# Four GNN layers on 64 graphs: recording the graphs as planned tasks, four in flight, with all compute engines tied to the planned order

## The chip, the cores and the metric

One core of a Trainium2 chip. The metric is the device time of one launch in microseconds (us); the executions of a kernel in one round agree within 0.4%, those of the kernel before within 0.6%, and each kernel was run four times or more beside the kernel before on the same chip. All runs quoted are of the fast state. TensorE is called PE in the profile, VectorE DVE, ScalarE ACT, GpSimd POOL and the sync queue SP.

## The reference, cut to what matters

Each of 64 graphs has 256 nodes with 512 features, a 256x256 adjacency and a node mask, all float32. Four layers follow each other, and each begins with a layer norm and a relu:

```python
h = max(layernorm(x), 0); x = x + w0 * (h @ Wv0)              # layer 0: w0 = softmax over nodes of a masked q.k sum
h = max(layernorm(x), 0); x = x + relu(att @ feats)           # layer 1: 8 heads; att = softmax over neighbours of
                                                              #   leaky_relu(e_self + e_neigh), masked by -1e10
h = max(layernorm(x), 0); x = x + relu(tanh(A*(Xc Xp^T)) Xp)  # layer 2: 8 heads
h = max(layernorm(x), 0); x = x + w3 * (h @ Wv3)              # layer 3: w3 = softmax over nodes again
```

The layers of one graph depend on each other, the graphs do not. So TensorE is fed by keeping several graphs in flight, each at another place of its four layers.

## The kernel before

Each graph is a Python generator. Three are in flight, and a loop lets each record a piece in turn. Pools hand out the tiles, and the scheduler then places every instruction by itself. The norm hops to GpSimd for the power -0.5, since VectorE does the rest of it; TensorE can transpose only when `hn` is there (cuts are marked `# ...`):

```python
def normed(xt):
    for c in range(NC): nc.vector.bn_stats(stats[:, c, :], xt[:, c, :])          # L165, VectorE
    for c in range(NC): nc.vector.bn_aggr(mv[:, c, :], stats[:, c, :])
    nc.vector.tensor_scalar(rstd, mv[:, :, 1], EPS, None, op0=OP.add)            # L169, VectorE, 128x2
    nc.gpsimd.tensor_tensor(rstd, rstd, power, OP.pow)                           # L170, GpSimd, 128x2
    for c in range(NC):                                                          # L173, VectorE
        nc.vector.tensor_scalar(hn[:, c, :], xt[:, c, :], mv[:, c, 0:1], rstd[:, c:c + 1],
                                op0=OP.subtract, op1=OP.mult)
    # ... TensorE transposes hn, ScalarE evicts it with a relu to ht
```

Layer 1: the sixteen row maxima, the sending of them, and then GpSimd's additions of the mask:

```python
for c in range(NC):
    for h in range(H):                                                           # L291, VectorE, 128x256 x16 a graph
        nc.vector.tensor_tensor_reduce(junk, en_b[:, h, :], neg[:, c, :], 1.0, -BIG, OP.add, OP.max, mx[:, c, h:h + 1])
    yield
# ... maxima transposed, sent to DRAM and broadcast to m_b
yield
for p in range(HP):
    for s in range(2):
        for j in range(NC):
            nc.scalar.activation(e[:, s, j, :], es_b[:, h, :], AF.Prelu, bias=..., alpha=0.2)
    nc.gpsimd.tensor_tensor(e, e, negt[:, None].to_broadcast([P, 2, NC, N]), OP.add)   # L340, GpSimd, 128x1024
    nc.vector.tensor_tensor(e, e, m_b[...], OP.subtract)                               # L341
    nc.scalar.activation(e, e, AF.Exp)
    # ... gather(): TensorE multiplies e by feats
    yield
```

## Time and profile before

| | before |
|---|---|
| median (range) | 5157.3 us (5156.8 to 5168.0) |
| TensorE busy, mean granted clock | 89%, 0.948 |
| VectorE, ScalarE, GpSimd busy | 52%, 33%, 24% |
| TensorE's waits for e (exponentials) and for hn (norms) | 257 and 113 us |

How to read it: TensorE is the bound, so only its idle time and its slow clock can be won. The prediction below shows those lines.

### The profile page before, as it was taken

What the parts mean: (1) busy time and instruction counts of PE and PEld (TensorE: products, weight loads), DVE (VectorE), ACT (ScalarE), POOL (GpSimd) and SP (SyncE); (2) the same over time, 40 slices, a digit from 0 to 9 for tenths busy, and PEclk for the clock granted to TensorE, in tenths of its full rate; (3) what the DMA queues carried; (4) which work ended last, traced back from release to release, by engine and by line L of the source; (5) the groups of instructions that cost most, each with busy time, mean ns of one, the idle gap of its engine ahead of it and who ended that gap; (6) DMA issues with size and microseconds to landing.
All of it is one profiled execution on the core that took longest, in us unless ns stands there. A gap on an engine that the chain in (4) does not pass through costs nothing.

```text
span 5153.0 us, 60457 instructions
## 1 busy us (share of the span) xinstructions
PE 4603.7 (89%) x22850; PEld 3120.2 (61%) x22850; DVE 2691.4 (52%) x7530; ACT 1679.7 (33%) x3333; POOL 1231.3 (24%) x1095
## 2 busy tenths in 40 slices
PE   4898998989999989989899999899898999899987
PEld 3665666666665656665666656566656666566665
DVE  3555555555555555555545555555555455555543
ACT  1323333233233233332332332333333323323322
POOL 1222222122122222221221222222212222222211
PEclk8999999999999999999999999999999999999988
DMA  4111211111112112111111121121111111111101
GB/s 121 61 56 53 72 37 72 62 63 56 57 52 72 60 49 72 40 69 64 61 56 59 50 72 60 49 72 40 69 64 61 56 64 48 69 64 45 65 29 37
DMA packets 99779, 306.88 MB, mean 60 GB/s; under 512 B 18016, under 2 KB 48800, under 8 KB 74912
## 3 DMA queue, kind: packets, MB, share of 16 engines
q1 hardware_dynamic: 74752, 261.65, 14.3%
q0 software_dynamic: 9216, 33.56, 1.7%
q10 hardware_dynamic: 15520, 7.80, 0.6%
q8 instruction: 181, 2.97, 0.2%
q14 instruction: 110, 0.90, 0.1%
HBM read 267.85 MB, written 35.13 MB: 59 GB/s over the span
## 4 chain that ended last, share of the span: by engine, by line
PE 38%; DVE 9%; POOL 4%; issue 4%; ACT 2%; DMA 0%; POOLq 0%; DVEq 0%; ACTq 0%
PE pf L187 9%; PE pv L187 9%; PE pz L433 5%; PE po L320 4%; POOL e L340 3%; PE pg L444 3%; PE pt L179 2%; DVE e L341 2%; DVE stats L165 1%; DVE junk L291 1%; PE pc L377 1%; DVE th L405 1%; ACT e L342 1%; PE pyt L391 1%; DVE xt L419 1%
## 5 line engine op out<-in xcount | busy, mean ns | idle before, releaser
L187 PE MATMUL pv<-wv_s,ht 128*128 128x512 f32 x2048 | 1005.8, 639 | 14.4 <-ACT ht L180 14.4
L320 PE MATMUL po<-feats,e 128*128 128x65 f32 x4096 | 574.4, 296 | 257.6 <-ACT e L342 257.0
L320 PEld LDWEIGHTS po<-feats,e 128*128 128x128 f32 x4096 | 549.0, 212 | 342.5 <-issue 216.9
L340 POOL TENSOR_TENSOR e<-e,negt 128x1024 f32<-128x1024 f32 x256 | 636.3, 2493 | 397.2 <-ACT e L338 311.3
L187 PEld LDWEIGHTS pv<-wv_s,ht 128*128 128x128 f32 x2048 | 403.5, 205 | 451.1 <-issue 426.0
L180 ACT ACTIVATE ht<-pt 128x512 f32<-128x512 f32 x512 | 287.2, 595 | 983.5 <-PE pt L179 982.8
L341 DVE TENSOR_TENSOR e<-e,m_b 128x1024 f32<-128x1024 f32 x256 | 362.6, 1431 | 376.9 <-POOL e L340 375.9
L338 ACT ACTIVATE e<-es_b,ec 128x256 f32<-128x256 f32 x1024 | 449.9, 495 | 46.5 <-PE po L320 37.8
L187 PE MATMUL pf<-w_s,ht 128*128 128x512 f32 x1024 | 452.3, 594 | 5.5 <-ACT ht L180 5.5
L433 PE MATMUL pz<-ht,m_s 128*128 128x256 f32 x2048 | 455.5, 381 | 0.7 <-ACT ht L180 0.7
L391 PE MATMUL pyt<-th,xp 128*64 128x256 f32 x2048 | 378.7, 404 | 66.9 <-ACT th L406 66.9
L433 PEld LDWEIGHTS pz<-ht,m_s 128*128 128x128 f32 x2048 | 387.6, 191 | 62.1 <-issue 10.4
L179 PE MATMUL pt<-ident,hn 128*128 128x128 f32 x2048 | 322.3, 302 | 113.2 <-DVE hn L173 112.9
L170 POOL TENSOR_TENSOR rstd<-rstd,power 128x2 f32<-128x2 f32 x256 | 199.0, 778 | 919.1 <-DVE mv L167 581.2
L406 ACT ACTIVATE th<-th 128x512 f32<-128x512 f32 x512 | 312.9, 623 | 305.8 <-DVE th L405 305.7
L405 DVE TENSOR_TENSOR th<-ps,adj_t 128x512 f32<-128x512 f32 x512 | 333.6, 683 | 103.3 <-PE ps L401 100.3
L179 PEld LDWEIGHTS pt<-ident,hn 128*128 128x128 f32 x2048 | 269.1, 160 | 193.3 <-issue 145.0
L342 ACT ACTIVATE e<-e 128x1024 f32<-128x1024 f32 x256 | 269.8, 1055 | 341.3 <-DVE e L341 339.5
L291 DVE CUSTOM_DVE_ANT_0 junk<-en_b,neg 128x256 f32<-128x256 f32 x1024 | 376.3, 420 | 4.5 <-DMA en_b<-er_d 3.0
L165 DVE BATCH_NORM_STATS2 stats<-xt 128x6 f32<-128x512 f32 x512 | 342.5, 678 | 56.2 <-POOL xt L331 51.1
L173 DVE TENSOR_SCALAR hn<-xt,mv,rstd 128x512 f32<-128x512 f32 x512 | 261.0, 548 | 172.1 <-POOL rstd L170 171.9
L331 POOL TENSOR_TENSOR xt<-xt,o 128x256 f32<-128x256 f32 x256 | 184.3, 727 | 611.5 <-DVE o L328 592.1
(88 smaller groups left out, 5239.6 us busy)
## 6 DMA issues: line engine op xcount, KB each, us to landing
en_b<-er_d SPq DMA_DIRECT2D x64, 1024.0 KB, 4.4
es_b<-er_d SPq DMA_DIRECT2D x64, 1024.0 KB, 6.7
m_b<-m_d SPq DMA_DIRECT2D x64, 1024.0 KB, 4.6
xt<-in_x_dram SPq DMA_DIRECT2D x64, 512.0 KB, 3.8
out_dram<-xt POOLq DMA_DIRECT2D x64, 512.0 KB, 3.2
adj_in<-in_adj_dram SPq DMA_DIRECT2D x64, 256.0 KB, 3.9
mask_in<-in_nodemask_dram SPq DMA_DIRECT2D x64, 128.0 KB, 8.1
w_n<-in_L_gnn_Wqk_dram ACTq DMA_DIRECT2D x16, 128.0 KB, 3.6
```

Source lines behind the costliest of these rows:

```text
L165: nc.vector.bn_stats(stats[:, c, :], xt[:, c, :])
L179: nc.tensor.transpose(pt[:, k * P:(k + 1) * P], hn[:, c, k * P:(k + 1) * P], ident)
L187: nc.tensor.matmul(p, ht[:, k, c * P:(c + 1) * P], w[:, k], start=(k == 0), stop=(k == KC - 1))
L291: nc.vector.tensor_tensor_reduce(junk, en_b[:, h, :], neg[:, c, :], 1.0, -BIG, OP.add, OP.max, mx[:, c, h:h + 1])
L320: nc.tensor.matmul(po[i][:, q, :], e[:, s, j, i * P:(i + 1) * P], feats[:, j, h, :], start=(j == 0), stop=(j == NC - 1))
L338: nc.scalar.activation(e[:, s, j, :], es_b[:, h, :], AF.Prelu, bias=ec[:, j, H + h:H + h + 1], alpha=0.2)
L340: nc.gpsimd.tensor_tensor(e, e, negt[:, None].to_broadcast([P, 2, NC, N]), OP.add)
L341: nc.vector.tensor_tensor(e, e, m_b[:, 2 * p:2 * p + 2, None, :].to_broadcast([P, 2, NC, N]), OP.subtract)
L342: nc.scalar.activation(e, e, AF.Exp)
L391: nc.tensor.matmul(pyt[s * U:(s + 1) * U, p % 2, :], xp[:, m, h * U:(h + 1) * U], th[:, s, m, :], start=(m == 0), stop=(m == NC - 1))
L405: nc.vector.tensor_tensor(th[:, s], ps[s], at, OP.mult)
L433: nc.tensor.matmul(pz[:, s, :], m3_s[:, k, d * P:(d + 1) * P], ht[:, k, :], start=(k == 0), stop=(k == KC - 1))
```

## The change

Its intent: let a planner, which knows about how long each step takes, decide what TensorE does next, so that with four graphs in flight a ready matmul is always at hand; and keep what it decided on TensorE, VectorE, ScalarE and GpSimd. Each graph is cut into tasks that name their predecessors, their steps (engine and length), the tiles taken and those given back. The core of the diff, with cuts:

```diff
-IN_FLIGHT = 3
-APART = 8
+IN_FLIGHT = 4
+BEHIND = 30.0
+PINNED = (mybir.EngineType.PE, mybir.EngineType.Activation, mybir.EngineType.DVE, mybir.EngineType.Pool,)
+    def issue(self, task, g, at):
+        # ... tiles are taken from the planner's own lists
+        task.run(*[t[2] for t in passing])
+        for i in traced[n:]:
+            if i.engine in PINNED:
+                if i.engine in self.last:
+                    self.tc.add_manual_dep(i, self.last[i.engine], ...NoSync...)
+                self.last[i.engine] = i.name
+        for engine, length in task.steps:
+            start = max(at, self.free[engine])
+            self.free[engine] = start + length
+    def run(self, graph, count):
+        # ... of all tasks whose predecessors are planned and whose tiles are there:
+        #     the one whose first step can start first; ties by graph and by the work left
+        @task(f"stats{layer}", after, [("V", 1.9), ("G", 0.75)])
+        @task(f"hn{layer}", f"stats{layer}", [("V", 1.1)], {"hn": 1})
+            @task(f"max{i}", f"<max{i - 1}" if i else "send neg", [("V", 2.0)], ...)     # four of these, four maxima each
+            @task(f"ea{p}", "wait negt" + ..., [("A", 2.0), ("G", 2.6)], ...)            # Prelu and GpSimd's addition
+            @task(f"eb{p}", f"ea{p} sendm", [("V", 1.21), ("A", 1.05)], ...)             # subtraction and exponential
-        nc.gpsimd.dma_start(out[b].rearrange("(c p) d -> p c d", p=P), xt)
+            nc.sync.dma_start(out[b].rearrange("(c p) d -> p c d", p=P), g["xt"])
```

## The prediction

> **What bounds the kernel now.** The page's first part gives the engines, its fourth the chain that ended last:
>
> ```profile
> PE 4603.7 (89%) x22850; PEld 3120.2 (61%) x22850; DVE 2691.4 (52%) x7530; ACT 1679.7 (33%) x3333; POOL 1231.3 (24%) x1095
> ...
> PE 38%; DVE 9%; POOL 4%; issue 4%; ACT 2%; DMA 0%; POOLq 0%; DVEq 0%; ACTq 0%
> ```
>
> TensorE is the bound and nothing else is near it; DMA is not on the chain. So the change can win only what TensorE loses. I read that from the timeline, in starts instead of ends, because ends are modelled:
>
> ```profile
> 2002.72 7.07 PE L433 MATMUL pz<-ht,m_s 128*128 128x256 f32 x32
> 2009.63 1.90 PE L320 MATMUL po<-feats,e 128*128 128x65 f32 x16
> 2011.36 1.04 PE L179 MATMUL pt<-ident,hn 128*128 128x128 f32 x8
> 2012.24 3.62 PE L444 MATMUL pg<-ht,zt 128*128 128x256 f32 x16
> ```
>
> From start to next start, undisturbed: pz 6.91 us for 32, po 1.73 for 16, eight transposes 0.88, pg 3.45. The same reading for every group gives a graph's full-speed work: pv of two layers 13.8, pf with w1a, w1b and w2 3.7 + 3.5 + 6.9, pz 6.9, pg 3.5, po 7.0, ps 4.3, pyt 4.1, all transposes into ht, xpt, y and adj 5.8, qk and first score 2.9, xc 1.9, small ones 0.9, together 65 us.
>
> The chain in order of time repeats every three graphs:
>
> ```profile
> 2226.28 8.76 PE pv L187 x16
> ...
> 2465.72 8.51 PE pv L187 x16
> ...
> 2701.79 8.23 PE pv L187 x16
> ```
>
> (2701.8 - 2226.3) / 6 = 79 us a graph. From 500 to 4900 us the windows view has TensorE busy 91%, so of 78.5 us some 71.3 are busy and 7.2 idle; the busy part is 6.4 us above the 65. That surplus is mostly clock, as windows of 3 us show (columns: stretch, its length, busy us of PE, PEld, DVE, ACT, POOL, then PEclk, DMA):
>
> ```profile
> 2088.00:2091.00 3.00, 1.55 (x15) 1.31 (x13) 2.99 (x7) 1.08 (x2) 0.00 (x0) 1.00 0.98 344
> 2091.00:2094.00 3.00, 0.29 (x2) 0.32 (x3) 2.28 (x10) 0.00 (x0) 0.69 (x1) 0.89 0.84 355
> 2094.00:2097.00 3.00, 2.31 (x6) 1.23 (x5) 3.00 (x16) 0.60 (x1) 0.00 (x0) 0.50 0.00 0
> 2097.00:2100.00 3.00, 3.00 (x5) 1.10 (x4) 2.97 (x19) 0.00 (x0) 0.36 (x1) 0.50 0.03 8
> 2100.00:2103.00 3.00, 3.00 (x11) 1.53 (x10) 1.64 (x5) 0.60 (x1) 0.92 (x2) 0.98 0.00 0
> ```
>
> A wait of 4.2 us (a transpose waiting for hn while VectorE works off y, two more normalisations and the row maxima) is followed by some 6 us at half clock. A mean clock of 0.948 means 10% of the span, some 540 us or 8.4 us a graph, at half; it costs up to 4 us a graph. So a wait is paid twice. The waits view names whom TensorE waits for:
>
> ```profile
> DVE e L341 <- POOL e L340: 375.9, 165, 4.9
> PE po L320 <- ACT e L342: 257.0, 123, 5.7
> PE pt L179 <- DVE hn L173: 112.9, 47, 8.6
> POOL out_dram L455 <- DVE xt L208: 712.7, 63, 24.7
> ```
>
> The exponentials of layer 1 (257 us) and the normalisations (113) are two thirds of its 549 us idle. The last line is GpSimd standing with a store at its head, unable to add the masks meanwhile.
>
> **What the Trainium skill says.** "TensorE: Matmul & The Clock Gate", part 1 on the clock gate: the array runs at full or half clock, half after an idle window of about 3.4 us. The windows above agree in kind. The same page, on engine queue depths: ScalarE and VectorE are strictly in order. So tying a compile-time order cannot speed an instruction; it decides who blocks whom. The store at GpSimd's head agrees. "Perfetto Trace Analysis", identifying the most-contended engine: matmul busy share is a poor measure of what is left. It agrees: 89% busy hides 6.4 us a graph. "DMA: Bandwidth & Descriptors", SWDGE vs HWDGE: plain transfers belong on the sync queue, whose descriptors hardware makes. Here the 64 issues took GpSimd 782 ns each.
>
> **The change, part by part.** Arithmetic is unchanged: no matmul, eviction or large transfer goes. A fourth graph enters, with four transposed adjacencies. The load broadcasts the node mask later, one memset of 127 ns a graph goes, and the store moves from GpSimd to the sync queue: 50 us of issue and most of the 713 us of standing leave GpSimd, which is 24% busy; alone worth little, since only waits for e pass through it.
>
> The large part is the order. A task puts all its instructions into the engines' orders when its first step is planned. An eviction is therefore fixed on VectorE when its matmul is issued, and VectorE-only work planned later stands behind it until that matmul ends. Before, the scheduler placed each instruction by itself. I listed the new order and walked three neighbouring graphs of its middle by hand, taking each group's undisturbed duration above and, for VectorE, the means of its rows (e 1.43 us or less, th 0.68, bn_stats 0.68, hn 0.55, four maxima 2.0), exponentials 1.06, GpSimd's e 2.5. This is an estimate, and leaves out most hand-over delays.
> - First graph: after the last po, VectorE has the division (1.2), stats of the newcomer (1.95), the y additions (1.4), two more stats (3.9) and half of hn (0.55): 9.0 us; TensorE has py, adj and y, 2.35 us. It stands 6.7 us. Later waits of 0.5 to 1.1 us; 70.5 us in all.
> - Second: the first subtraction of e stands on VectorE behind the eviction of the last w1b group, and po follows that group at once: 0.4 + 1.4 + 1.1 and hand-overs are 3.3 us of wait; 69 us.
> - Third: the last th stands behind a division and stats (1.8 us), then hn behind maxima (1.1), and po twice behind e; 75.5 us.
>
> The mean is 71.7 us: 65 of work and about 7 of wait. So the plan does not remove the waits; it breaks them up. The three have two waits long enough for half clock, against 90 half-clock stretches for 64 graphs before, over four for three graphs. I take 2 us a graph of clock loss (two stretches of 6 us, half of it lost, over three graphs) and 1.5 us for hand-overs, a choice: some 10 a graph on the path at 0.15. That gives 75.2 us. Start and end now take 5153 - 64 x 78.5 = 129 us; the setup is the same, with four graphs ready behind it, so I keep 100. Sum: 64 x 75.2 + 100 = 4910 us; I lean 30 us lower because the broadcasts, which the walk found with at least 4 us of slack, and the removed store may help: **4880 us**.
>
> **Rivals.**
> 1. VectorE's order becomes the bound. For: 52% busy, and 55% in a run of 4880 us (2691 / 4880); evictions block it while some 35 us of matmuls a graph run. Against: TensorE's groups without eviction there (pv, transposes, po, pyt) leave about 30 us for 29 us of VectorE-only work. If it tips, 78 us a graph: 5090, no gain.
> 2. Pinned orders are brittle: a broadcast later than planned, or a store ahead of a send in the sync queue (a load waits there for a store to land), stops VectorE and then all. For: four engines can't step around it. Against: row maxima came 11 to 15 us after their send in the walk, and about 7 are needed (1.4 + 4.4 + issue). If wrong, 2 to 4 us a graph more: 5040 to 5170.
> 3. TensorE fills: with four graphs a ready matmul nearly always exists, waits fall to 3 us, the clock stays full: 65 + 3 + 1.5 = 69.5, or 4550. For: long matmul stretches of two graphs interleave. Against: the walk's 6.7 us hole, where all four graphs stand at a layer boundary.
>
> **Range and chances.** The walk is good to some 2.5 us a graph, 160 us, mostly through clock and hand-overs: 4690 to 5060 at 8 in 10. Faster by 2% means under 5054: 0.87. Within 2%: 0.10, by the first or second rival. Slower: 0.03; it needs over 80 us a graph.
>
> **What would show it.** TensorE's matmul counts unchanged. Period near 75 us; mean clock about 0.97 (4 us of 75 at half); TensorE busy 91 to 94%. The wait of po for the exponentials falls well below 257 us; the wait of transposes for hn does not fall, and may exceed 113 us. GpSimd's wait for the store goes. If the clock reads 0.99 and the hn wait is short, the walk was too dark (third rival). If TensorE waits for evictions, or VectorE for broadcasts, the first or second rival took it.

## More of the kernel before

The kernel before read 5157 to 5172 us in the rounds, which were on different chips, so a difference between kernels of different rounds is good to some 15 us.

The next lines are from the views of two source lines of the kernel before; the three figures are the shortest, the median and the longest of one instruction, in ns.

```profile
L291 DVE CUSTOM_DVE_ANT_0 junk<-en_b,neg x1024: 403/418/2571, 93.2 to 5046.9; 128x256 f32<-128x256 f32 x171
L340 POOL TENSOR_TENSOR e<-e,negt x256: 2327/2360/3420, 97.5 to 5059.3; 128x1024 f32<-128x1024 f32 x128
```

A row maximum takes 418 ns and one addition of the mask 2360 ns. The longest maximum, 2571 ns, is an addition long. In the kernel before that happened to one of the 1024.

## The result, and the profile after

The changed kernel took 5066.9 us (5066.8 to 5068.1, four runs) against 5157.3: a ratio of 0.982, with an interval of 0.9803 to 0.9837. Ratios here are the mean time of one kernel's fast runs over that of the other's of the same rounds, so not quite the ratio of the medians quoted. That is 1.8% faster, and 187 us above the predicted 4880 and 7 us above the predicted range.

The page of the changed kernel, the lines that answer to the first ones of the prediction:

```profile
PE 4492.2 (89%) x22850; PEld 3094.1 (61%) x22850; DVE 3072.8 (61%) x7530; ACT 1698.9 (34%) x3333; POOL 1173.8 (23%) x969
...
PE 79%; DVE 17%; issue 2%; ACT 1%; DMA 1%; ACTq 0%; POOL 0%; DVEq 0%; POOLq 0%
```

TensorE has the same 22850 matmuls and is no fuller than before. VectorE has the same 7530 instructions and is busy for 381 us more (3073 against 2691). Nobody gave it work; its instructions became longer. (Its 17% of the chain can't be set against the 9% in the prediction: that chain reaches back only to 2178 us and covers 57% of its span.) The waits view (total us, times, longest):

```profile
PE tr L378 <- DVE hn L370: 397.6, 87, 13.5
PE acc L551 <- ACT pair L534: 64.0, 32, 10.4
```

The waits for exponentials fell from 257 to 64 us as meant, and those of the transposes for hn rose from 113 to 398. The gain was given back there: TensorE is idle for 573 us in all, where it was 549. The 90 us that the kernel did win lie in its busy time, 4492 us against 4604, and no run separates where they come from. The period can be read from the chain in order of time, in which one group (line L668) returns once a graph:

```profile
1687.12 6.91 PE tr L668 x32
...
4472.41 6.91 PE tr L668 x32
```

There are 36 graphs between the two, so 77.4 us a graph against 78.5 before and 75.2 predicted. (64 x 77.4 leaves some 112 us of the span for start and end.)

Which VectorE instructions grew? By form, the maxima, hn and the 128x2 addition ahead of the power, first before, then after; columns are busy us, mean ns, idle before:

```profile
L291 DVE CUSTOM_DVE_ANT_0 junk<-en_b,neg 128x256 f32<-128x256 f32 x1024 | 376.3, 420 | 4.5 <-DMA en_b<-er_d 3.0
L173 DVE TENSOR_SCALAR hn<-xt,mv,rstd 128x512 f32<-128x512 f32 x512 | 261.0, 548 | 172.1 <-POOL rstd L170 171.9 <-PE pt L179 0.2
L169 DVE TENSOR_SCALAR rstd<-mv 128x2 f32<-128x2 f32 x256 | 66.7, 261 | 3.0
```

```profile
L490 DVE CUSTOM_DVE_ANT_0 junk<-all,neg 128x256 f32<-128x256 f32 x1024 | 644.1, 684 | 0.0
L370 DVE TENSOR_SCALAR hn<-xt,mv,rstd 128x512 f32<-128x512 f32 x512 | 327.6, 682 | 13.5 <-POOL rstd L364 8.0 <-PE tr L378 5.2
L363 DVE TENSOR_SCALAR rstd<-mv 128x2 f32<-128x2 f32 x256 | 143.0, 559 | 8.9
```

Those three grew by 268, 67 and 76 us. The views of single lines (shortest, median, longest in ns) say how:

```profile
L490 DVE CUSTOM_DVE_ANT_0 junk<-all,neg x1024: 406/418/2587, 103.2 to 4943.5; 128x256 f32<-128x256 f32 x171
L526 POOL TENSOR_TENSOR pair<-pair,negt x256: 2327/2358/3337, 108.7 to 4936.7; 128x1024 f32<-128x1024 f32 x128
L359 DVE BATCH_NORM_STATS2 stats<-xt x512: 667/677/695, 4.9 to 5032.4; 128x6 f32<-128x512 f32 x171
```

The median maximum is unchanged at 418 ns. A count over the records of the trace gives 165 of the 1024 above 600 ns, some half of those near 2.5 us, where the kernel before has one. Every one of the 165 ends within 0.3 us of the end of a GpSimd instruction: 110 with an addition of the mask, 50 with the product `am` (L681, 1.44 us), 5 with others. bn_stats, with one tensor in, never changed. The timeline of the longest hole shows the meeting; these lines are from 2286 to 2301 us:

```profile
2293.36 2.33 POOL L526 TENSOR_TENSOR pair<-pair,negt 128x1024 f32<-128x1024 f32 x1
...
2293.55 2.17 DVE L363 TENSOR_SCALAR rstd<-mv 128x2 f32<-128x2 f32 x1
...
2296.58 2.36 POOL L526 TENSOR_TENSOR pair<-pair,negt 128x1024 f32<-128x1024 f32 x1
...
2296.67 2.55 DVE L490 CUSTOM_DVE_ANT_0 junk<-all,neg 128x256 f32<-128x256 f32 x1
2298.90 1.44 POOL L681 TENSOR_TENSOR am<-adj,mask_in 128x512 f32<-128x512 f32 x1
...
2300.68 1.54 PE L378 MATMUL tr<-ident,hn 128*128 128x128 f32 x6 [13.47 <-DVE hn L370]
```

An addition of two columns, 170 ns as a rule, begins 0.2 us after GpSimd's addition and ends with it, 2.17 us later. A maximum does the same 3 us on: it begins 0.1 us after an addition and ends 0.3 us after it. TensorE stands 13.5 us, and the windows of 3 us show what follows (columns as in the prediction):

```profile
2289.00:2292.00 3.00, 0.00 (x0) 0.00 (x0) 2.93 (x9) 3.00 (x9) 3.00 (x2) 0.71 0.12 46
2292.00:2295.00 3.00, 0.00 (x0) 0.00 (x0) 2.96 (x6) 0.68 (x2) 3.00 (x4) 0.50 0.00 0
...
2301.00:2304.00 3.00, 3.00 (x16) 3.00 (x15) 2.37 (x11) 1.66 (x3) 0.00 (x0) 0.52 0.49 131
2304.00:2307.00 3.00, 3.00 (x16) 2.66 (x15) 0.00 (x0) 0.73 (x2) 0.00 (x0) 1.00 0.00 0
```

VectorE reads as full (2.9 of 3 us) through the whole hole. A busy share does not tell an engine that works from one that stands inside an instruction. The three microseconds after the hole run at half clock; over the run, the mean clock fell from 0.948 to 0.934.

Two pages of the Trainium skill that I had not looked up for the prediction state the mechanism. "SBUF — State Buffer", in "SBUF: two separate sides", says that VectorE and GpSimd share a pair of ports under an exclusive lock: a VectorE instruction with two SBUF inputs, or one in a two-port mode, and a GpSimd instruction exclude each other for the whole of the one that began first. "GPSIMD Engine Reference", in its specifications, says that they share these interfaces. The trace agrees: 418 ns, or as long as what is left of a GpSimd instruction. Whether this is what cost the time is for the experiments.

### The profile page after: what moved, and what is told of

Read it like the earlier page. It is cut to its first block, busy times and chain, and to the rows that moved or that the text cites. A ratio compares the mean times of both kernels' runs of the same rounds, so it can differ in the third digit from the quotient of the medians.

```text
span 5065.2 us, 60793 instructions
## 1 busy us (share of the span) xinstructions
PE 4492.2 (89%) x22850; PEld 3094.1 (61%) x22850; DVE 3072.8 (61%) x7530; ACT 1698.9 (34%) x3333; POOL 1173.8 (23%) x969
## 4 chain that ended last, share of the span: by engine, by line
PE 79%; DVE 17%; issue 2%; ACT 1%; DMA 1%; ACTq 0%; POOL 0%; DVEq 0%; POOLq 0%
PE tr L309 20%; PE acc L309 16%; PE acc L551 10%; PE tr L668 9%; PE tr L378 5%; PE tr L618 5%; DVE junk L490 5%; PE tr L690 4%; PE acc L639 4%; DVE stats L359 3%; DVE hn L370 2%; PE tr L602 2%; DVE rstd L363 2%; DVE pair L621 1%; PE tr L587 1%
## 5 line engine op out<-in xcount | busy, mean ns | idle before, releaser
L309 PE MATMUL acc<-wv_s,ht 128*128 128x512 f32 x2048 | 978.5, 623 | 0.2
L490 DVE CUSTOM_DVE_ANT_0 junk<-all,neg 128x256 f32<-128x256 f32 x1024 | 644.1, 684 | 0.0
L309 PEld LDWEIGHTS acc<-wv_s,ht 128*128 128x128 f32 x2048 | 392.4, 201 | 411.4 <-issue 400.3
L526 POOL TENSOR_TENSOR pair<-pair,negt 128x1024 f32<-128x1024 f32 x256 | 612.7, 2407 | 118.1 <-issue 69.2
L551 PE MATMUL acc<-feats,pair 128*128 128x65 f32 x4096 | 544.0, 292 | 64.0 <-ACT pair L534 64.0
L551 PEld LDWEIGHTS acc<-feats,pair 128*128 128x128 f32 x4096 | 522.3, 208 | 118.2 <-ACT pair L534 81.7
L668 PE MATMUL tr<-ht,m_s 128*128 128x256 f32 x2048 | 463.8, 381 | 0.0
L309 PE MATMUL tr<-w_s,ht 128*128 128x512 f32 x1024 | 460.8, 595 | 0.1
L668 PEld LDWEIGHTS tr<-ht,m_s 128*128 128x128 f32 x2048 | 385.4, 191 | 73.1 <-issue 25.6
L524 ACT ACTIVATE pair<-all,ec 128x256 f32<-128x256 f32 x1024 | 419.7, 496 | 14.5 <-DMA all<-er_d 9.7
L370 DVE TENSOR_SCALAR hn<-xt,mv,rstd 128x512 f32<-128x512 f32 x512 | 327.6, 682 | 13.5 <-POOL rstd L364 8.0
```

The source lines that it names most:

```text
L309: nc.tensor.matmul(p, ht[:, k, c * P:(c + 1) * P], w[:, k], start=(k == 0), stop=(k == KC - 1))
L370: nc.vector.tensor_scalar(g["hn"][:, c, :], g["xt"][:, c, :], st["mv"][:, c, 0:1], st["rstd"][:, c:c + 1], op0=OP.subtract, op1=OP.mult)
L490: nc.vector.tensor_tensor_reduce(junk, g["all:en"][:, h, :], g["neg"][:, c, :], 1.0, -BIG, OP.add, OP.max, st["mx"][:, c, h:h + 1])
L524: nc.scalar.activation(e[:, s, j, :], g["all:es"][:, h, :], AF.Prelu, bias=st["ec"][:, j, H + h:H + h + 1], alpha=0.2)
L526: nc.gpsimd.tensor_tensor(e, e, g["negt"][:, None].to_broadcast([P, 2, NC, N]), OP.add)
L551: nc.tensor.matmul(po[i][:, h % 4, :], e[:, s, j, i * P:(i + 1) * P], feats[:, j, h, :], start=(j == 0), stop=(j == NC - 1))
```

## The experiments

The theories. **A**: the stretched VectorE instructions lie in TensorE's path at the layer boundary and cost the missing time. **B**: they lie beside it; the hole comes from VectorE's order alone, as the hand walk had it. **C**: tying four engines costs by itself. Later came **D**: tying costs only where the plan's lengths are false; and **E** against **F**, on where the rest of the gain came from.

### e1_later_adds: additions planned behind the maxima

```diff
-            @task(f"ea{p}", "wait negt" + (f" <ea{p - 1}" if p else ""), [("A", 2.0), ("G", 2.6)], ...
+            @task(f"ea{p}", "wait negt max0 max1 max2 max3" + (f" <ea{p - 1}" if p else ""), [("A", 2.0), ("G", 2.6)], ...
```

> One dependency more in the plan: the four Prelu-and-mask tasks of a graph wait for its four tasks of row maxima, so that GpSimd's additions can no longer run beside the same graph's maxima (exact result). Theory A (VectorE's instructions with two SBUF inputs stand still while a GpSimd addition runs; the maxima rose from 420 to 684 ns and that sits in the path at the layer boundary): maxima back below 460 ns, VectorE's busy time down from 3073 to about 2800 us, the wait of the transposes for hn from 398 to under 250 us, time 4850 to 4950 us. Theory B (the hole at the layer boundary comes from VectorE's order alone, as the walk had it): within 1% of 5067 us. Theory C (tying the engines is what hurts): within 1% of 5067 us.

Correct, and 4577.2 us: ratio 0.8853 (0.8830 to 0.8876), 490 us below the changed kernel. B and C had expected no change, and A some 120 to 220 us, so none of them is the whole of it. The same groups and waits, and the page's first line:

```profile
PE 4332.7 (95%) x22850; PEld 2977.7 (65%) x22850; DVE 2764.0 (60%) x7530; ACT 1699.4 (37%) x3333; POOL 1190.6 (26%) x969
```

```profile
L490 DVE CUSTOM_DVE_ANT_0 junk<-all,neg 128x256 f32<-128x256 f32 x1024 | 377.5, 425 | 0.1
```

```profile
PE tr L378 <- DVE hn L370: 111.8, 65, 7.4
```

The maxima are back at 425 ns, the waits for hn at 112 us, and the clock is 0.990. But this edit also gave a wholly new order, and that may be where the time went, so it does not rule B out. The next two runs keep the changed kernel's order.

### e2_short_add: the same orders, GpSimd's addition cut short

```diff
-                nc.gpsimd.tensor_tensor(e, e, g["negt"][:, None].to_broadcast([P, 2, NC, N]), OP.add)
+                nc.gpsimd.tensor_tensor(e[:, :, :, :2], e[:, :, :, :2], g["negt"][:, None, :, :2].to_broadcast([P, 2, NC, 2]), OP.add)
```

> GpSimd's mask addition is cut to 2 of 256 columns (wrong result on purpose); the orders of TensorE, VectorE and ScalarE are those of the changed kernel, instruction for instruction. Theory A: no VectorE instruction is stretched any more (maxima 420 ns, the 128x2 addition in rstd 261 instead of 559 ns, hn 548 instead of 682), VectorE busy about 2650 us, time 4780 to 4900 us. Theory B: 5000 us or more, since TensorE waits for the exponentials only 64 us in all and gains little from an earlier addition.

4875.7 us, 191 us below the changed kernel with TensorE's, VectorE's and ScalarE's orders instruction for instruction the same (the result is wrong). B had 5000 us or more, so it falls as the whole cause. The page's first line, the maxima and the waits for hn:

```profile
PE 4473.1 (92%) x22850; PEld 3089.2 (63%) x22850; DVE 2691.5 (55%) x7530; ACT 1696.3 (35%) x3333; POOL 617.7 (13%) x969
```

```profile
L490 DVE CUSTOM_DVE_ANT_0 junk<-all,neg 128x256 f32<-128x256 f32 x1024 | 405.6, 453 | 0.1
```

```profile
PE tr L378 <- DVE hn L370: 227.2, 65, 8.3
```

With the orders unchanged, VectorE's busy time fell from 3073 to 2692 us, so 381 us of stretching came from the long additions. That this is just what VectorE had gained is partly chance: 33 maxima still stand, up to 1493 ns, 31 of them beside the product `am`. The time won is half of the 381 us, so about half was in TensorE's path. A holds, with one reserve: GpSimd was also relieved of its additions, so e was there sooner. TensorE's waits for e did not shorten (68 us against 64).

### e3_one_input_max: maxima with one SBUF input

```diff
-                    nc.vector.tensor_tensor_reduce(junk, g["all:en"][:, h, :], g["neg"][:, c, :], 1.0, -BIG,
-                                                   OP.add, OP.max, st["mx"][:, c, h:h + 1])
+                    nc.vector.tensor_reduce(st["mx"][:, c, h:h + 1], g["all:en"][:, h, :], AX.X, OP.max)
```

> The row maxima read one SBUF tile instead of two (a plain reduction, wrong result on purpose); all else, the orders and GpSimd's additions too, as in the changed kernel. Theory A: the reductions take about 420 ns and are not stretched though the additions run beside them, time 4900 to 4980 us (268 of the some 410 us of stretching are the maxima's, part of it may pass to hn and rstd, which still meet the additions). Theory B: within 1% of 5067 us.

4995.7 us, 71 us below the changed kernel, just past the slow end of the expectation (4980). (Its maximum is over all nodes instead of neighbours; the softmax does not depend on it.) The outputs are right. Two lines of the single-line views and of the groups say both why it helped and why so little:

```profile
L490 DVE TENSOR_REDUCE mx<-all x1024: 399/408/421, 103.5 to 4872.0; 128x1 f32<-128x256 f32 x171
```

```profile
L370 DVE TENSOR_SCALAR hn<-xt,mv,rstd 128x512 f32<-128x512 f32 x512 | 393.6, 811 | 13.6 <-POOL rstd L364 8.0 <-PE tr L378 5.2
L363 DVE TENSOR_SCALAR rstd<-mv 128x2 f32<-128x2 f32 x256 | 160.6, 627 | 8.9
```

With the additions running as before, no one-input maximum of 1024 took over 421 ns. So it was the instruction with two inputs that stood. But hn went from 682 to 811 ns: what stood behind the maxima now meets the additions itself.

### e4_unpinned: no engine tied

```diff
-PINNED = (mybir.EngineType.PE, mybir.EngineType.Activation, mybir.EngineType.DVE, mybir.EngineType.Pool,)
+PINNED = ()
```

> The plan still allots the tiles and the order in which tasks are recorded, but no engine is tied to it: the scheduler of before places each instruction by itself. Theory C (pinned orders are brittle, tying all four engines costs): faster than 4990 us. Theories A and B: no faster than 5020 us; I expect 5050 to 5200 us.

4858.6 us, 208 us below the changed kernel; my expectation, 5050 to 5200, missed. In the changed kernel, tying costs 4%. The clash was not gone (maxima at 631 ns, hn at 900), but in the scheduler's order TensorE ran into it less: the waits for hn were 80 us, though some for other tiles came up. So C is right here. What remained was whether it is right in general.

### e5_later_unpinned: e1_later_adds with no engine tied

> The plan of e1_later_adds, with no engine tied. Theory D (tying costs only where the plan's lengths are wrong, as with the additions beside the maxima; with those apart the planned order is the better one): slower than e1_later_adds's 4577, 4620 to 4850 us. Theory C (tying costs by itself, as the 208 us between e4_unpinned and the changed kernel suggest): faster than 4560 us.

4690.6 us, 113 us above e1_later_adds. So tying loses 208 us with one plan and wins 113 with another that differs in one dependency, which fits D. Untied, the scheduler brings some of the clash back (maxima at 551 ns against 425), and how much of the 113 us is that clash was not tested: no untied run was free of it. That a tied order is as good as the lengths it was planned with is a reading of these two pairs, not shown.

### e8_short_replanned: e2_short_add, and the plan told of it

```diff
-            @task(f"ea{p}", "wait negt" + (f" <ea{p - 1}" if p else ""), [("A", 2.0), ("G", 2.6)], ...
+            @task(f"ea{p}", "wait negt" + (f" <ea{p - 1}" if p else ""), [("A", 2.0), ("G", 0.3)], ...
```

> e2_short_add (addition cut to 2 columns, wrong result on purpose), and the plan told so: the addition's length in it 0.3 instead of 2.6 us. So no addition stands ahead of a normalisation in GpSimd's order, in the plan or on the chip. Theory E (the 300 us by which e1_later_adds beats e2_short_add come from the plan's placing GpSimd's long additions ahead of the normalisations' power, which makes it hold hn back behind the maxima): 4560 to 4680 us. Theory F (they come from the sixteen Prelu activations or the buffers of the pairs, which e1_later_adds also moves): 4800 us or more.

4712.1 us (wrong result): 164 us below e2_short_add, between what E and F expected. The waits for hn are 111 us, as in e1_later_adds. So the plan made with long additions puts the norms late even where the additions stretch nothing, which fits E; but the edit changes the whole order, and it is not as fast as e1_later_adds.

### e9_rstd_vector: the norm without the hop to GpSimd

```diff
-            @task(f"stats{layer}", after, [("V", 1.9), ("G", 0.75)])
+            @task(f"stats{layer}", after, [("V", 2.1)])
-                nc.gpsimd.tensor_tensor(rstd, rstd, power, OP.pow)
+                nc.vector.reciprocal(rstd, rstd)
```

> The changed kernel with the normalisation's power replaced by a reciprocal on VectorE (wrong result on purpose: 1/v for 1/sqrt(v)), in the plan too. The additions still run beside the maxima. Theory E: hn no longer waits for GpSimd, time 4650 to 4850 us. Theory F: above 4950 us.

5229.9 us, slower than both kernels, where E had expected a large gain (1/v for 1/sqrt(v) is wrong; the power itself did not compile on VectorE). So taking the hop to GpSimd away does not help by itself. The groups suggest why:

```profile
L370 DVE TENSOR_SCALAR hn<-xt,mv,rstd 128x512 f32<-128x512 f32 x512 | 459.9, 948 | 0.0
L490 DVE CUSTOM_DVE_ANT_0 junk<-all,neg 128x256 f32<-128x256 f32 x1024 | 385.6, 431 | 0.0
```

In the new order the maxima are almost clear of the additions (431 ns), and hn is in their midst, at 948 ns. hn is what TensorE waits for, and those waits rose to 628 us. So the clash moved to a worse place. As the whole order changed too, what part of the 163 us above the changed kernel it cost is not shown, and E itself stays untested by this run.

### e6_three and e12_later_three: three graphs in flight

```diff
-IN_FLIGHT = 4
+IN_FLIGHT = 3
```

> The changed kernel with three graphs in flight in place of four. If the fourth graph earns its place, 5150 us or slower; if the holes come from the order alone, within 1.5% of 5067 us. The maxima would be stretched as before (over 550 ns), since nothing in the plan keeps them from the additions.

> e1_later_adds with three graphs in flight in place of four. If the fourth graph matters once the clash is gone: 4650 us or slower (e6_three lost 4% of the changed kernel); if three fill TensorE in a sound order: within 1.5% of 4577 us.

On the changed kernel 5288.4 us, 4.4% above it. On e1_later_adds 5124.9 us, 12% above it. Both plans lose by going to three graphs, but the second figure is not its worth alone: with three, the plan brought the additions beside hn again (1101 ns, maxima at 424), a clash that its one dependency does not exclude.

### e11_split_add: the addition cut into four

```diff
-                nc.gpsimd.tensor_tensor(e, e, g["negt"][:, None].to_broadcast([P, 2, NC, N]), OP.add)
+                for s, j in ((0, 0), (0, 1), (1, 0), (1, 1)): nc.gpsimd.tensor_tensor(e[:, s, j], e[:, s, j], g["negt"][:, j], OP.add)
```

> The changed kernel with each GpSimd addition of 128x1024 cut into four of 128x256 (exact result; the same orders on TensorE, VectorE and ScalarE). Theory A, as the runs have it so far: a VectorE instruction that meets an addition stands until that one instruction ends, so the stretched maxima shorten from 1.4 and 2.5 us to about 1 us or less, their mean falls from 684 to below 560 ns, and the time falls to 4920 to 5040 us although GpSimd's additions grow from 613 to some 720 us in all. If instead the two engines merely share bandwidth, the sum of stretching stays (mean near 684 ns) and the time does not fall.

Correct, and 4918.5 us: 148 us below the changed kernel, a little better than expected, with the same orders, although GpSimd's additions grew from 613 to 793 us:

```profile
L490 DVE CUSTOM_DVE_ANT_0 junk<-all,neg x1024: 411/423/1491, 103.2 to 4797.7; 128x256 f32<-128x256 f32 x171
L526 POOL TENSOR_TENSOR pair<-pair,negt x1024: 712/740/1718, 107.5 to 4794.1; 128x256 f32<-128x256 f32 x171
```

The count over the trace's records gives 339 stretched maxima instead of 165, but most last about 0.93 us (318 of them less than 1 us) instead of up to 2.5; the mean fell to 597 ns, not below the 560 that I had written. More GpSimd work, in shorter pieces, gave a faster kernel. Sharing of bandwidth would not do that; standing until one instruction ends does. Unlike e2_short_add, this run does not relieve GpSimd, so that run's reserve does not carry the result.

### e7_before_sync_store: the store alone

```diff
-        nc.gpsimd.dma_start(out[b].rearrange("(c p) d -> p c d", p=P), xt)
+        nc.sync.dma_start(out[b].rearrange("(c p) d -> p c d", p=P), xt)
```

> The kernel before with one part of the change alone: the store on the sync queue instead of GpSimd's. The prediction called it worth little: within 1.5% of 5157 us; GpSimd's 713 us of standing at the store are gone from the waits. If waiting stores had held the exponentials back, 3% faster or more.

The kernel before with this one part: 5181.0 us, ratio 1.0013 (0.9988 to 1.0038). Nothing, as predicted. GpSimd's 713 us at the store turned into waits elsewhere (for the maxima ahead of `neg` alone 805 us, where it was 212).

### e13_later_split: e1_later_adds with the addition cut into four

> e1_later_adds (additions planned behind the maxima) with each addition cut into four, in search of the best version. e1_later_adds still shows hn at 613 against 548 ns, so some 30 us of stretching are left, and little of it in the path; GpSimd gains some 110 us of work. Theory A: within 1% of 4577 us. If GpSimd has become limiting there: 4620 us or slower.

Correct, 4581.9 us, ratio 0.8864 (0.8848 to 0.8880): the same as e1_later_adds within the intervals. With the additions out of the way, cutting them brings nothing. e1_later_adds stays the best version, 11.5% below the kernel before and 9.7% below the changed one.

## Why the prediction was right or wrong

- **The bound and what could be won**: right. TensorE's idle time and clock were all that could be won, and e1_later_adds won it, at 95% busy and a clock of 0.990.
- **The step that failed**: "taking each group's undisturbed duration above and, for VectorE, the means of its rows (e 1.43 us or less, th 0.68, bn_stats 0.68, hn 0.55, four maxima 2.0)". Those rows were measured in an order that kept GpSimd's additions away from the maxima; the walk then used them in an order that put both side by side. In it, a maximum was 684 ns, hn 682, the addition in rstd 559, and VectorE was busy for 381 us more, 6.0 us a graph. With the additions cut short in the same order (e2_short_add) 191 us came back: 5067 became 4876. A sign of it was in the profile before: e, whose mean of 1.43 us the walk used, has a median of 1.23, since 42 of its 256 were stretched there too.
- **That e2_short_add meets the predicted 4880 is luck.** TensorE's busy share in the middle of the run (the first busy time in the two lines below, of the changed kernel and of e2_short_add), the period of L668 and the clock records give what each term of the walk came to:

```profile
500.00:4900.00 4400.00, 3954.13 (x20234) 2724.81 (x20232) 2719.90 (x6657) 1506.37 (x2958) 1039.30 (x853) 0.94 0.17 60
```

```profile
500.00:4700.00 4200.00, 3908.65 (x20028) 2698.88 (x20027) 2351.64 (x6603) 1488.27 (x2927) 541.68 (x843) 0.95 0.18 62
```

| us a graph | the walk | changed kernel | e2_short_add | e1_later_adds |
|---|---|---|---|---|
| period | 75.2 | 77.4 | 74.5 | 69.5 |
| TensorE idle (walk: 6.7 of waits, 1.5 of hand-overs) | 8.2 | 7.8 | 5.2 | 2.5 |
| lost to half clock (half of the busy time spent in it) | 2.0 | 2.8 | 2.7 | 0.0 |
| the rest of the busy time: the work at full speed | 65 | 66.7 | 66.6 | 66.9 |

Without the stretching, the walk's waits were 3.0 us too long, its work 1.6 and its clock loss 0.7 too small, and these almost cancel. The stretching then added 2.9 us, most of it as idle time, which is why the changed kernel's idle time looks like the predicted one. (Ends of matmuls are modelled, so part of the last row may be idle time.) Of the 187 us, 139 are the period, 30 the lean to 4880, and some 12 start and end (112 us against 100).
- **Two readings of the kernel before** were too generous. Its busy surplus of 6.4 us a graph was called mostly clock; half of its 6.3 us of busy time at half clock is 3.2, so the other half was not clock; e1_later_adds, hardly ever at half clock, still has 66.9 us. And the chain shown covers only the last 57% of the span.
- **The holes**: the walk's hole at the layer boundary is there. The waits for hn were to stay or exceed 113 us and were 398; those for exponentials were to fall well below 257 and were 64. Of the hole's length the walk had 6.7 us; the longest was 13.5 us, and 8.3 us in e2_short_add. TensorE was 89% busy at a clock of 0.934, against 91 to 94% and about 0.97 in the prediction.
- **The first rival** had the right time (5090, the run 5067) for another reason: VectorE was not blocked by evictions but by GpSimd, within its instructions. **The second rival**, brittle orders, was right in kind: untying gave 208 us here. But it was not a late broadcast (the subtraction of e waited 21 us in all for it); what the runs found is two engines that exclude each other, which the plan counts as independent. **The third**, TensorE filled at 4550 us, is almost what e1_later_adds reached.
- **The small parts**: the store alone is worth nothing (e7_before_sync_store).
- **Where the gain went**: most of it was turned into a new wait. 193 us less waiting for exponentials were paid with 285 us more for hn.
- **Open**: of the 490 us between the changed kernel and e1_later_adds, the stretching by the additions explains 191 with the order kept (148 in e11_split_add, where the work stays). Telling the plan of short additions took 164 more. The last 135, from e8_short_replanned to e1_later_adds, show largely as clock (283 us at half against 94 us, by the clock records, which can cost up to 95 us) with equal waits for hn; which of the moved tasks does it was not tested.

## What to carry to other kernels

Durations from a profile hold for the order in which they were taken: before reusing them for a new order, look at the shortest and the longest of a group, and ask which other engine's instruction the long ones are as long as. A planner or a hand-tied order must know which VectorE and GpSimd instructions exclude each other, here the maxima with two SBUF inputs, hn and the addition in rstd on one side. One dependency that kept the maxima clear of the additions, with the new order that came of it, was worth 490 us here; the stretching alone was worth 191. Whether tying engines to a plan pays depends on the plan: the same tie lost 208 us with one and won 113 with another. And when a run meets a predicted number, check the terms of the sum: here three errors cancelled.

## What the Trainium skill lacked or had wrong

- "SBUF — State Buffer", SBUF: two separate sides: the exclusive lock is as stated (418 ns or up to 2587 beside additions of 2358; one input: never over 421). hn (537 ns, stretched to 2650) and the 128x2 addition of a constant (170 ns, stretched to 2178) read one tensor each; the section lists their operation, tensor_scalar, among those that can enter a two-port mode, so they are no exception to it. No trace here shows the mode that they ran in.
- The same page's remedies for two engines that exclude each other are a matter of what is scheduled when; it does not name cutting the GpSimd instruction. In four pieces, that took 148 us off the kernel although GpSimd's additions grew from 613 to 793 us.
- No page that I read says that the standing shows as busy: VectorE read 2.9 to 3.0 of 3 us in a hole in which TensorE stood for 13.5 us.
- "TensorE: Matmul & The Clock Gate", part 1: half clock after idle windows agrees (0.50 in the hole and 0.52 in the 3 us after it). It has no formula for the loss from the lengths of the waits: 41 waits of over 3.4 us in the changed kernel went with 72 stretches and 674 us at half clock by the clock records, 40 in e2_short_add with 57 and 495 us, and 8 in e1_later_adds with 11 and 94 us.
